# A two-batch product in the fill of a conditioned-residual kernel, with rank terms added in PSUM

## The chip, the cores and the metric

The kernel runs on one core of one Trainium2 chip. The metric is device time in microseconds (us) of one launch, as a median of runs. A profiled execution also has a span, from its first to its last instruction.

## What is computed

For each of 8 batches the reference builds a 512 x 512 matrix from a conditioning row and adds two residual layers to x (1024 x 512 per batch). Cut to what matters:

```python
h = gelu(layernorm(cond) @ w1 + b1)
x_a, x_b = split(h @ w2 + b2)                  # each (8, 512, RANK=8)
layer = base_layer + einsum('bdr,bkr->bdk', x_a, x_b)
x1 = x + (x + x @ layer)                       # first layer and its residual
ys = cond / sqrt(512)
d = rsqrt(ys**2 @ weight**2 + eps)
out = x1 + (x1 * ys) @ weight * d              # second layer and its residual
```

The kernel folds both layers into one matrix for each batch, P_b = (2I + base + A_b B_b) N_b with N_b = I + diag(ys_b) weight diag(d_b), and computes out_b = x_b P_b. Every product is done in fp32r with each factor as a rounded head and a remainder, so one product is three matmuls: head by head, head by remainder, remainder by head.

## The kernel before, in words

The work has two stages. In the **fill**, the P of the first batches is made while w2 (16 MB) streams in. In the **main** stage, 48 output tiles of batches 0 to 5 are made, twelve matmuls each, with other work hung on numbered tiles; batches 6 and 7 follow in a closing stage.

**The part of P without its rank term**, called q here, is (2I + base) N_b: 512 x 512 x 512, 48 matmuls of 128 x 512 for one batch. `Base` (lines 524-545) does it plainly: 16 units of three matmuls, and ScalarE copies each finished PSUM bank into `q[b]`. The class `Fill` (695-715) runs batches 1, 2 and 3 in this way (batch 0 was done ahead, `first_base`). `Pair` (547-643) makes q of two batches at once with seven products of half-size blocks in place of eight: 14 units of six matmuls for two batches. Its right operands are sums of blocks of N_b and N_b+1 (`sums`), rounded on ScalarE and completed on VectorE (`round`, `finish`); its left operands are sums of blocks of 2I + base^T, made by `left_sum` for products 5, 6, 3 and 7 (368-379). Before the change batches 4 and 5, and the parts for 6 and 7, use it from the main stage, and `left_sum` runs at the end of the fill (lines 800 to 804).

**What q still lacks.** Batch 0 was started before d was known, so `q[0]` holds only (2I + base) diag(ys) weight diag(d), and the identity's share of N_0 is missing: `twice_i_plus_base` and `add_base` (476-483) add 2I + base, from a copy of base (1 MB, `b_nat`), to `q[0]` on VectorE. Then the rank term: a matmul of two folded factors lands in a PSUM bank, and VectorE adds the bank to q: `rank_first` (497-501) for batch 0, `rank_term` (514-522) for the others, which first needs the folded factors loaded by eight small DMAs from POOL's queue (`load_rank`, 505-512). Then `split_p` (651-657) writes the head `ph` (ScalarE) and the remainder `pl` (VectorE) of P.

**x.** `load_x` brings half a batch (1 MB, SP's queue). `split_x` (667-674) cuts it in pieces of 256 columns: head on ScalarE, remainder on VectorE. Output tile t of the main stage uses piece t // 2, and its third matmul is the first to read the remainder (`main`, 811-821).

**What sets the order.** Matmuls keep their program order throughout (`mm`, line 44). In the fill, VectorE, ScalarE and SP keep theirs too (`InOrder`, 52-64), so the list in lines 717 to 805 is an order written by hand for each of these queues; after `InOrder.on = False` (805) their instructions are placed by the scheduler of the framework. POOL's DMAs are placed by it everywhere. In the main loop (1003-1014) `at(place, f)` hangs work behind tile number `place`. `rank_t` (435-470) is a generator: each `next(steps)` issues one step of the chain for the factor B. `w2_group` (389-403) loads 1 MB of w2 and issues eight matmuls of 32 columns with it.

**Buffers.** PSUM has four `acc` banks, two `misc` banks and two `px` banks in the fill; the last four become the `po` banks of the main stage when `setup` closes (807). Tiles of 1 MB share nine slots called `big`. Right operands share two slots each for heads (`nh`) and remainders (`nl`).

Of the kernel before, what the change touches and what calls it, by code (L numbers as in the profile page):

```python
# [30 lines left out]
def cond_resid_kernel(ctx: ExitStack, tc: tile.TileContext, small, cond, condrows, consts,  # L31
# [99 lines left out]

    def right_tiles(name):

        h = npool.tile([P, 2, D], F32R, tag="nh", name=f"nh_{name}")
        l = npool.tile([P, 2, D], F32R, tag="nl", name=f"nl_{name}")
        return h, l

    right0 = [right_tiles(f"0_{j}") for j in range(2)]
# [194 lines left out]
    def n_half(b, j):  # L333

        n = npool.tile([P, 2, D], F32, tag="n", name=f"n_{b}_{j}", bufs=4)
        for kk in range(2):
            k = 2 * j + kk
            ve.scalar_tensor_tensor(n[:, kk, :], w_sb[:, k, :], ysT[:, k, b:b + 1],
                                           d_all[b], ALU.mult, ALU.mult)
            blk = n[:, kk, k * P:(k + 1) * P]  # L340
            ve.tensor_add(blk, blk, ident)
        return n

    def round_right(n, name, wide=True):
# [20 lines left out]
    a11, a21 = b_raw[:, 0:2, 0:HD], b_raw[:, 0:2, HD:D]  # L365
    a12, a22 = b_raw[:, 2:4, 0:HD], b_raw[:, 2:4, HD:D]

    def left_sum(i):
        if i == 5:
            sraw["s"] = big_tile("sraw").rearrange("p k (u i) -> p k u i", u=2)  # L370
        s1, s2, s3, s4 = (sraw["s"][:, u] for u in range(4))
        s, x, y, op = {5: (s1, a21, a22, ve.tensor_add), 6: (s2, s1, a11, ve.tensor_sub),
                       3: (s4, a12, s2, ve.tensor_sub), 7: (s3, a11, a21, ve.tensor_sub)}[i]
        op(s, x, y)
        h = cp.tile([P, 2, HD], F32R, name=f"sh_{i}")
        l = cp.tile([P, 2, HD], F32R, name=f"sl_{i}")
        se.copy(h, s)
        ve.tensor_sub(l, s, h.bitcast(F32))
        left[i] = h, l

    b_nat = []


    px = [xps.tile([P, D], F32, name=f"px_{h}") for h in range(2)]
# [4 lines left out]
    def w2_group():  # L389
        h, r, k = todo.pop(0)  # L390
        t = big_tile(f"w2_{h}_{r}_{k}")
        sy.dma_start(t, w2[h, r, k])
        if len(todo) == 15:
            sy.dma_start(cst, consts)
        if len(todo) == 8:
            sy.dma_start(crow, condrows)
            sy.dma_start(b2r, b2rows)
        if len(todo) == 6:
            b_nat.append(big_tile("b_nat"))
            sy.dma_start(b_nat[0], base)  # L400
        for j in range(4):
            mm(px[h][32 * j:32 * j + 32, :], hT[:, k, r, :], t[:, j, :],
               start=(r == 0 and k == 0), stop=(r == 1 and k == KC - 1))
# [69 lines left out]

        ve.tensor_mul(q[b][:, c, :], q[b][:, c, :], d_all[b])

    def twice_i_plus_base():
        for c in range(KC):
            blk = b_nat[0][:, c, c * P:(c + 1) * P]
            ve.scalar_tensor_tensor(blk, ident, 2.0, blk, ALU.mult, ALU.add)

    def add_base(b):
        for c in range(KC):
            ve.tensor_add(q[b][:, c, :], q[b][:, c, :], b_nat[0][:, c, :])

    def round_w(k):
        se.copy(wh[:, k, :], w_sb[:, k, :])
# [7 lines left out]
        tm[0] = sp.tile([P, D], F32R, name="tm_0")  # L494
        ve.tensor_scalar_mul(tm[0], stt[0].bitcast(F32), mask[:, 0:1])

    def rank_first(c):

        ps = misc.tile([P, D], F32, tag="misc", name=f"pr_0_{c}")
        mm(ps, sa[0][:, c * P:(c + 1) * P], tm[0], start=True, stop=True)  # L500
        ve.tensor_add(q[0][:, c, :], ps, q[0][:, c, :])

    fold = {}

    def load_rank(b):

        for name in ("a", "t"):
            g, i = divmod(b, 4)
            fold[name, b] = npool.tile([P, D], F32R, tag=f"f{name}", name=f"f{name}_{b}", bufs=2)
            for c in range(KC):  # L510
                nc.gpsimd.dma_start(fold[name, b][32 * c:32 * c + 32, :],  # L511
                                    kept[name, g][32 * i:32 * i + 32, :])

    def rank_term(b):

        ps = [acc.tile([P, D], F32, tag="acc", name=f"pr_{b}_{c}") for c in range(KC)]
        for c in range(KC):
            at = slice(32 * c, 32 * c + 32)
            mm(ps[c], fold["a", b][at, c * P:(c + 1) * P], fold["t", b][at, :],
               start=True, stop=True)  # L520
        for c in range(KC):
            ve.tensor_add(q[b][:, c, :], ps[c], q[b][:, c, :])

    class Base:

# [21 lines left out]
    class Pair:  # L547
# [60 lines left out]
                    mm(bank, a[:, kk, at], m[:, kk, :], start=(first and kk == 0 and i == 0),  # L608
                       stop=(kk == 1 and i == 2), skip_group_check=not first)

        def unit(self):
            p, s = self.todo.pop(0)
            b, w, z = self.b, ("w", s), ("z", s)
            key = w if p in (1, 6, 7, 4) else z
            first = p in (1, 5, 2)
            if first:
                self.bank[key] = acc.tile([P, D], F32, tag="acc", name=f"pp_{b}_{p}_{s}")
            if (p, s) in ((1, 0), (6, 0)):
                i = b + (p == 6)
                q[i] = big_tile(f"q_{i}")  # L620
            bank = self.bank[key]
            self.product(p, s, bank, first)
            c11, c21 = q[b][:, s, :], q[b][:, 2 + s, :]
            c12, c22 = (q[b + 1][:, s, :], q[b + 1][:, 2 + s, :]) if b + 1 in q else (None, None)
            if p == 1:
                se.copy(c11, bank)
            elif p == 5:
                se.copy(c21, bank)
            elif p == 6:
                se.copy(c12, bank)  # L630
            elif p == 3:
                ve.tensor_add(c12, bank, c12)
            elif p == 7:
                se.copy(c22, bank)
                ve.tensor_add(c22, c22, c21)
            elif p == 2:
                ve.tensor_add(c11, bank, c11)
            else:
                se.copy(c21, bank)
# [27 lines left out]
    def split_x(b, j, part=None):  # L667
# [3 lines left out]
            xs[b, j] = big.tile([P, 2, KC, 2 * P], F32R, tag="big", name=f"xs_{b}_{j}")  # L671
            se.copy(xs[b, j][:, 0], t)
        if part != 0:
            ve.tensor_sub(xs[b, j][:, 1], t, xs[b, j][:, 0].bitcast(F32))


    stt, sa = [None, None], [None, None]
# [14 lines left out]
    bcast_d(0)  # L692
    first_base(3, (1, 2, 3))

    class Fill:


        def __init__(self):
            self.bases = [Base(b) for b in (1, 2, 3)]
            self.ns, self.rests = {}, {}  # L700

        def units(self, count):
            for _ in range(count):
                if self.bases[0].at == 4 * KC:
                    self.bases.pop(0)
                self.bases[0].units(1)

        def make_n(self, b, j):
            self.ns[b, j] = n_half(b, j)

        def round(self, b, j):
            self.rests[b, j] = round_right(self.ns[b, j], f"{b}_{j}", b == 3)

        def finish(self, b, j):
            next(f for f in self.bases if f.b == b).add(self.rests[b, j]())

    fill = Fill()
    fill.make_n(1, 0)
    fill.round(1, 0)
    fill.make_n(1, 1)  # L720
    keep_first((0, 1))
    fill.round(1, 1)
    keep_first((2, 3))
    fill.finish(1, 0)
    for c in range(2):
        times_d(0, c)
    fill.finish(1, 1)
    for c in range(2, KC):
        times_d(0, c)
    w2_group()  # L730
    w2_group()
    for k in range(2, KC):
        round_w(k)
    fill.units(4)
    for k in range(2, KC):
        rest_w(k)
    fill.make_n(2, 0)
    w2_group()
    w2_group()
    fill.units(4)  # L740
    fill.round(2, 0)
    fill.make_n(2, 1)
    fill.finish(2, 0)
    w2_group()
    w2_group()
    fill.units(6)
    w2_group()
    steps = rank_t()
    next(steps)
    w2_group()  # L750
    next(steps)
    fill.units(4)
    w2_group()
    next(steps)
    w2_group()
    fill.units(2)
    fill.round(2, 1)
    next(steps)
    fill.finish(2, 1)
    next(steps)  # L760
    fill.units(3)
    twice_i_plus_base()
    w2_group()
    next(steps)
    w2_group()
    next(steps)
    mask_t()
    add_base(0)
    fill.units(2)
    fill.make_n(3, 0)  # L770
    next(steps)
    w2_group()
    w2_group()
    next(steps)
    fill.units(2)
    w2_group()
    load_x(0, 0)
    xa = (split(with_bias(0)),)
    fill.round(3, 0)
    fill.units(4)  # L780
    done = stack(xa, neg_a, "a", 0)
    fill.finish(3, 0)
    sa[0] = done()
    fill.units(3)
    fill.make_n(3, 1)
    p_tiles(0)
    rank_first(0)
    rank_first(1)
    fill.round(3, 1)
    fill.units(2)  # L790
    split_p(0, 0, 0)
    rank_first(2)
    rank_first(3)
    split_p(0, 0, 1)
    fill.finish(3, 1)
    split_p(0, 1)
    split_x(0, 0)
    fill.units(4)
    sa[1] = stack(xa, neg_a, "a", 1)()
    left_sum(5)  # L800
    fill.units(8)
    split_x(0, 1)
    for p in (6, 3, 7):
        left_sum(p)
    InOrder.on = False

    setup.close()
    po = ctx.enter_context(tc.tile_pool(name="po", bufs=4, space=PSUM))
    pools = {"o": making.enter_context(tc.tile_pool(name="opool", bufs=4))}

    def main(b, t):
        s = xs[b, t // 2]
# [149 lines left out]

    pairs = {}
    place = lambda i: divmod(i, NTT)
    for b in range(1, 4):
        first = (b - 1) * NTT
        at(*place(max(0, 3 * b - 7)), load_rank, b)
        at(*place(3 * b - 1), rank_term, b)
        for j in range(2):
            at(*place(first + 3 + j), split_p, b, j)  # L970

    for b, spots in ((4, [11 + 3 * n // 4 for n in range(14)]), (6, [24 + 2 * n // 3 for n in range(14)])):
        first, end = spots[0], spots[-1] + 1
# [118 lines left out]
```

## Time and profile before

| | us |
|---|---|
| median of 3 runs (301.88 to 302.4) | 301.93 |
| the profiled execution | 302.08 |
| its span | 300.3 |
| matmuls of the fill's batches 1 to 3, first start | 26.68 |
| first matmul of the main stage | 80.35 |
| first matmul of the closing stage | 254.59 |

Matmul durations overlap in the profile: a matmul of 128 x 512 is listed with 0.39 to 0.40 us, and the next starts 0.23 us after it. Instructions of VectorE and ScalarE overlap by some 0.1 us in the same way, so queues are added up here by the distance of starts. "PE" is TensorE, "DVE" VectorE, "ACT" ScalarE.

### The profile page before, as it was taken

How to read it: one execution, taken by the hardware profiler on the slowest of the kernel's cores; microseconds unless marked ns; L12 is line 12 of the kernel's file. 1: busy time of each engine (PE TensorE's matmuls, PEld its weight loads, DVE VectorE, ACT ScalarE, POOL GpSimd, SP SyncE). 2: the span in 40 equal slices, each digit the busy share in tenths (PEclk: the TensorE clock that was granted, in tenths of full speed). 3: DMA queues.
4: the chain of work that ended last, by engine and by line, in shares of the span. 5: the costliest groups of instructions: out<-in, count | busy, mean ns of one | idle time of the engine just before them, and what ended most of it. 6: DMA issues, size and time to landing. Idle time of an engine off the chain costs nothing.

```text
span 300.3 us, 4005 instructions
## 1 busy us (share of the span) xinstructions
PE 293.4 (98%) x1501; PEld 227.1 (76%) x1501; DVE 211.0 (70%) x312; ACT 154.1 (51%) x226; POOL 34.8 (12%) x74
## 2 busy tenths in 40 slices
PE   7999999999999999999999999999999999999995
PEld 2655465466877778888887888888778888998995
DVE  4779840979569999935869994366562996479722
ACT  4757132256566673647634463656442663663630
POOL 0011000057004551000003600000000000000000
PEclk9999999999999999999999999999999999999999
DMA  7999999696619984605513841524516785131234
GB/s 210 410 428 419 405 424 419 219 326 183 197 70 305 306 288 126 239 35 210 204 43 97 230 164 46 201 55 192 210 70 210 244 267 227 38 140 49 93 140 142
DMA packets 19524, 62.14 MB, mean 207 GB/s; under 512 B 2720, under 2 KB 4000, under 8 KB 15152
## 3 DMA queue, kind: packets, MB, share of 16 engines
q1 hardware_dynamic: 6896, 39.57, 35.7%
q10 hardware_dynamic: 8832, 15.99, 14.2%
q0 software_dynamic: 3776, 6.31, 8.0%
q8 instruction: 12, 0.20, 0.3%
q14 instruction: 8, 0.07, 0.1%
HBM read 44.02 MB, written 17.84 MB: 206 GB/s over the span
## 4 chain that ended last, share of the span: by engine, by line
PE 84%; DVE 9%; ACT 3%; DMA 2%; issue 1%; SPq 0%; ACTq 0%
PE po L45 44%; PE pp L45 13%; PE pq L45 10%; PE sw L45 5%; PE px L45 4%; PE sz L45 2%; PE pg L45 2%; DVE n L62 2%; DMA b_raw<-in_baseT 2%; DVE sraw L62 1%; PE pr L45 1%; PE sv L45 1%; ACT o L62 1%; DVE sl L62 1%; ACT sh L62 1%
## 5 line engine op out<-in xcount | busy, mean ns | idle before, releaser
L45 PE MATMUL po<-ph,xs 128*128 128x512 f32 x384 | 123.8, 392 | 0.0
L45 PEld LDWEIGHTS po<-ph,xs 128*128 128x128 f32 x384 | 72.1, 188 | 16.8 <-issue 1.7
L45 PE MATMUL po<-pl,xs 128*128 128x512 f32 x192 | 74.8, 389 | 0.0
L62 ACT COPY o<-po 128x512 f32<-128x512 f32 x48 | 28.1, 586 | 52.8 <-PE po L45 52.8
L45 PEld LDWEIGHTS po<-pl,xs 128*128 128x128 f32 x192 | 36.1, 188 | 7.4
L62 DVE TENSOR_TENSOR xs<-x,xs 128x1024 fp32r<-128x1024 f32 x24 | 29.0, 1221 | 10.5 <-ACT xs L62 10.4
L62 ACT CAST xs<-x 128x1024 fp32r<-128x1024 f32 x24 | 24.9, 1052 | 3.7 <-DMA x<-in_x 1.9
L62 DVE TENSOR_TENSOR nl_p<-n,nh_p 128x1024 fp32r<-128x1024 f32 x14 | 17.1, 1222 | 12.3 <-ACT nh_p L62 12.2
L62 DVE TENSOR_TENSOR pl<-q,ph 128x1024 fp32r<-128x1024 f32 (+1 forms) x16 | 18.3, 1153 | 6.2 <-ACT ph L62 6.1
L62 DVE TENSOR_TENSOR q<-pr,q 128x512 f32<-128x512 f32 x32 | 20.1, 682 | 3.5 <-PE pr L45 3.5
L511 POOL DMA_DIRECT2D fa<-kept_a x28 | 13.7, 502 | 64.9 <-PE pr L45 64.8
L45 PE MATMUL pq<-nh,bh 128*128 128x512 f32 x48 | 19.8, 412 | 0.0
L45 PE MATMUL pq<-nl,bh 128*128 128x512 f32 x48 | 19.1, 398 | 0.1
L45 PE MATMUL pq<-nh,bl 128*128 128x512 f32 x48 | 19.0, 395 | 0.0
L62 DVE SCALAR_TENSOR_TENSOR n<-w_sb,ysT,d 128x512 f32<-128x512 f32 x24 | 17.7, 745 | 1.2 <-DMA d<-d_out 1.2
L62 ACT CAST nh_p<-n 128x1024 fp32r<-128x1024 f32 x14 | 14.8, 1054 | 6.3 <-PE pp L45 5.5
L62 ACT COPY o<-sw 128x512 f32<-128x512 f32 (+1 forms) x15 | 7.5, 500 | 19.2 <-PE sw L45 14.4
L62 ACT CAST ph<-q 128x1024 fp32r<-128x1024 f32 (+1 forms) x16 | 15.8, 1001 | 1.2 <-DVE q L62 0.8
L45 PE MATMUL px<-w,hT 128*32 128x512 f32 x128 | 16.0, 601 | 0.0
L62 ACT COPY q<-pp 128x512 f32<-128x512 f32 x20 | 11.7, 587 | 7.7 <-PE pp L45 7.7
L45 PEld LDWEIGHTS pq<-nh,bh 128*128 128x128 f32 x48 | 9.0, 188 | 8.4 <-issue 5.0
L511 POOL DMA_DIRECT2D ft<-kept_t x28 | 13.8, 509 | 5.2 <-DMA kept_t<-st_t 5.0
(185 smaller groups left out, 515.1 us busy)
## 6 DMA issues: line engine op xcount, KB each, us to landing
w<-in_w SPq DMA_DIRECT2D x16, 1024.0 KB, 10.5
x<-in_x SPq DMA_DIRECT2D x16, 1024.0 KB, 5.4
out<-o ACTq DMA_DIRECT2D x48, 256.0 KB, 3.2
out<-o ACTq DMA_DIRECT2D x6, 512.0 KB, 2.9
ft<-kept_t POOLq DMA_DIRECT2D x28, 64.0 KB, 3.4
fa<-kept_a POOLq DMA_DIRECT2D x28, 64.0 KB, 2.9
d<-d_out POOLq DMA_DIRECT2D x6, 256.0 KB, 5.2
w_sb<-in_weight SPq DMA_DIRECT2D x2, 512.0 KB, 5.3
```

The lines of the kernel that those rows point to most:

```text
L45: tc.keep_in_program_order(nc.tensor.matmul(*args, **kw))
L62: return lambda *a, **kw: pin(f(*a, **kw)) if InOrder.on else f(*a, **kw)
L511: nc.gpsimd.dma_start(fold[name, b][32 * c:32 * c + 32, :], kept[name, g][32 * i:32 * i + 32, :])
```

## The change

- **Batches 2 and 3** are made by `Pair(2)` in place of two `Base`. Twelve of its 14 units are in the fill, the last two (product 4) behind output tiles 1 and 2 of the main stage. All sums for the left operands are made in the middle of the fill (`left_raw`, `left_rest`). Two kinds of additions on VectorE can be put off with `unit(hold)`.
- **Right operands** have three slots in place of two.
- **Batch 0's base** is added by a DMA from POOL's queue that accumulates into `q[0]`; the copy `b_nat` and four additions on VectorE go.
- **Rank terms of batches 0, 1 and 2**: ScalarE copies q into the PSUM bank (`seed`), the matmul adds onto it, and `take` splits P straight out of the bank (head on ScalarE, remainder on VectorE). Addition into q and `split_p` go for these batches. Batch 3 keeps the old way. The rank terms of batches 1, 2 and 3 hang behind tiles 3, 9 and 6 (before: 2, 5 and 8), their loads behind 0, 4 and 1 (before: 0, 0 and 2). The folded factors get a pool of their own, opened when the fill ends.
- **Pieces 1 to 3 of batch 0's x**: the remainder is made by ScalarE writing minus the head, and an accumulating DMA from POOL's queue adding x from DRAM.
- `n_half` adds the identity to both of its blocks in one instruction.

The core of the diff:

```diff
-        h = npool.tile([P, 2, D], F32R, tag="nh", name=f"nh_{name}")
-        l = npool.tile([P, 2, D], F32R, tag="nl", name=f"nl_{name}")
+        h = npool.tile([P, 2, D], F32R, tag="nh", name=f"nh_{name}", bufs=3)
+        l = npool.tile([P, 2, D], F32R, tag="nl", name=f"nl_{name}", bufs=3)
...
-            blk = n[:, kk, k * P:(k + 1) * P]
-            ve.tensor_add(blk, blk, ident)
+        blk = n.rearrange("p k (c i) -> p (k c) i", i=P)[:, 2 * j:2 * j + 6:5, :]
+        ve.tensor_add(blk, blk, ident.unsqueeze(1).to_broadcast([P, 2, P]))
...
+    def add_base():
+
+        blk = q[0].rearrange("p k (c i) -> p (k c) i", i=P)[:, 0:16:5, :]
+        ve.scalar_tensor_tensor(blk, ident.unsqueeze(1).to_broadcast([P, KC, P]), 2.0, blk,
+                                ALU.mult, ALU.add)
+        nc.gpsimd.dma_start(q[0], base, accum_op=ALU.add)
...
+    def seed(b, c, ps):
+        se.copy(ps, q[b][:, c, :])
+    def take(b, c, ps):
+        se.copy(ph[b][:, c, :], ps)
+        ve.tensor_sub(pl[b][:, c, :], ps, ph[b][:, c, :].bitcast(F32))
+    def onto(ps, a, t):
+        mm(ps, a, t, start=False, stop=True, skip_group_check=True)
...
+            hi, lo = xs[b, j][:, 0], xs[b, j][:, 1]
+            if b == 0 and j:
+                se.mul(lo, hi.bitcast(F32), -1.0)
+                nc.gpsimd.dma_start(lo, x[b, j // 2][:, :, (j % 2) * 2 * P:(j % 2 + 1) * 2 * P],
+                                    accum_op=ALU.add)
...
+    two = Pair(2)
+    two.make_n(1)
     w2_group()
     w2_group()
-    fill.units(4)
+    base1.units(4)
+    two.round(1)
+    two.make_n(2)
+    two.round(2)
+    left_raw(5)
+    two.finish(1)
+    left_raw(6)
+    left_rest(5)
+    left_raw(7)
+    left_raw(3)
+    left_rest(6)
+    add_base()
...
+    bank = [px[1], misc.tile([P, D], F32, tag="misc", name="pr_0_1")]
+    p_tiles(0)
+    for c in range(2):
+        seed(0, c, bank[c])
+    two.unit()
+    two.finish(3)
     w2_group()
     load_x(0, 0)
     xa = (split(with_bias(0)),)
+    two.units(2)
     done = stack(xa, neg_a, "a", 0)
+    bank.append(px[0])
+    seed(0, 2, bank[2])
+    two.round(7)
     sa[0] = done()
+    bank.append(misc.tile([P, D], F32, tag="misc", name="pr_0_3"))
+    seed(0, 3, bank[3])
+    two.finish(7)
+    held = []
+    two.unit(held)
+    for c in range(KC):
+        rank_first(c, bank[c])
+        take(0, c, bank[c])
     split_x(0, 0)
+    two.unit(held)
+    two.unit(held)
+    two.unit(held)
     sa[1] = stack(xa, neg_a, "a", 1)()
+    two.round(4)
+    two.finish(4)
+    for f in held:
+        f()
     split_x(0, 1)
-    for p in (6, 3, 7):
-        left_sum(p)
     InOrder.on = False
...
+    at(*place(1), two.unit)
+    at(*place(2), two.unit)
+    for b, load, spot in ((1, 0, 3), (3, 1, 6), (2, 4, 9)):
+        at(*place(load), load_rank, b)
+        at(*place(spot), rank_term, b, b < 3)
+    for j in range(2):
+        at(*place(19 + j), split_p, 3, j)
```

More of the change, by code (lines that the diff above doesn't have):

```diff
@@ L366, in cond_resid_kernel, with left_raw @@
     a12, a22 = b_raw[:, 2:4, 0:HD], b_raw[:, 2:4, HD:D]
-    def left_sum(i):
+    def left_raw(i):
         if i == 5:
@@ L375, in left_sum, with left_rest @@
         h = cp.tile([P, 2, HD], F32R, name=f"sh_{i}")
+        se.copy(h, s)
+        sraw[i] = s, h
+    def left_rest(i):
+        s, h = sraw[i]
         l = cp.tile([P, 2, HD], F32R, name=f"sl_{i}")
-        se.copy(h, s)
         ve.tensor_sub(l, s, h.bitcast(F32))
         left[i] = h, l
-    b_nat = []
     px = [xps.tile([P, D], F32, name=f"px_{h}") for h in range(2)]
@@ L397, in w2_group @@
             sy.dma_start(b2r, b2rows)
-        if len(todo) == 6:
-            b_nat.append(big_tile("b_nat"))
-            sy.dma_start(b_nat[0], base)
         for j in range(4):
@@ L474, in times_d @@
         ve.tensor_mul(q[b][:, c, :], q[b][:, c, :], d_all[b])
[L476 to L483, printed above, removed]
+    def add_base():
[3 more added lines that the diff above has]
+        nc.gpsimd.dma_start(q[0], base, accum_op=ALU.add)
     def round_w(k):
@@ L495, in mask_t, with rank_first @@
         ve.tensor_scalar_mul(tm[0], stt[0].bitcast(F32), mask[:, 0:1])
[L497 to L503, printed above, removed]
+    def seed(b, c, ps):
[5 more added lines that the diff above has]
+        mm(ps, a, t, start=False, stop=True, skip_group_check=True)
+    def rank_first(c, ps):
+        onto(ps, sa[0][:, c * P:(c + 1) * P], tm[0])
+    fold, pools = {}, {}
     def load_rank(b):
@@ L508, in load_rank @@
             g, i = divmod(b, 4)
-            fold[name, b] = npool.tile([P, D], F32R, tag=f"f{name}", name=f"f{name}_{b}", bufs=2)
+            fold[name, b] = pools["fold"].tile([P, D], F32R, tag=f"f{name}", name=f"f{name}_{b}", bufs=2)
             for c in range(KC):
@@ L512, in load_rank, with rank_term @@
                                     kept[name, g][32 * i:32 * i + 32, :])
-    def rank_term(b):
+    def rank_term(b, take_p=False):
         ps = [acc.tile([P, D], F32, tag="acc", name=f"pr_{b}_{c}") for c in range(KC)]
+        if take_p:
+            for c in range(KC):
+                seed(b, c, ps[c])
         for c in range(KC):
             at = slice(32 * c, 32 * c + 32)
-            mm(ps[c], fold["a", b][at, c * P:(c + 1) * P], fold["t", b][at, :],
-               start=True, stop=True)
+            a, t = fold["a", b][at, c * P:(c + 1) * P], fold["t", b][at, :]
+            if take_p:
+                onto(ps[c], a, t)
+            else:
+                mm(ps[c], a, t, start=True, stop=True)
         for c in range(KC):
-            ve.tensor_add(q[b][:, c, :], ps[c], q[b][:, c, :])
+            if take_p:
+                take(b, c, ps[c])
+            else:
+                ve.tensor_add(q[b][:, c, :], ps[c], q[b][:, c, :])
     class Base:
@@ L609, in product, with unit @@
                        stop=(kk == 1 and i == 2), skip_group_check=not first)
-        def unit(self):
+        def unit(self, hold=None):
             p, s = self.todo.pop(0)
@@ L630, in unit @@
                 se.copy(c12, bank)
+            elif p == 3 and hold is not None:
+                hold.append(lambda: ve.tensor_add(c12, bank, c12))
             elif p == 3:
@@ L634, in unit @@
                 se.copy(c22, bank)
-                ve.tensor_add(c22, c22, c21)
+                if hold is not None:
+                    hold.append(lambda: ve.tensor_add(c22, c22, c21))
+                else:
+                    ve.tensor_add(c22, c22, c21)
             elif p == 2:
@@ L673, in split_x @@
         if part != 0:
-            ve.tensor_sub(xs[b, j][:, 1], t, xs[b, j][:, 0].bitcast(F32))
+            hi, lo = xs[b, j][:, 0], xs[b, j][:, 1]
[3 more added lines that the diff above has]
+                                    accum_op=ALU.add)
+            else:
+                ve.tensor_sub(lo, t, hi.bitcast(F32))
     stt, sa = [None, None], [None, None]
@@ L693, in cond_resid_kernel, with round1 @@
     first_base(3, (1, 2, 3))
[L695 to L720, printed above, removed]
+    base1, n1 = Base(1), {}
+    def round1(j):
+        n1[j] = round_right(n1[j], f"1_{j}", False)
+    n1[0] = n_half(1, 0)
+    round1(0)
+    n1[1] = n_half(1, 1)
     keep_first((0, 1))
-    fill.round(1, 1)
+    round1(1)
     keep_first((2, 3))
-    fill.finish(1, 0)
+    base1.add(n1[0]())
     for c in range(2):
         times_d(0, c)
-    fill.finish(1, 1)
+    base1.add(n1[1]())
     for c in range(2, KC):
@@ L733, in cond_resid_kernel @@
         round_w(k)
-    fill.units(4)
+    base1.units(4)
     for k in range(2, KC):
         rest_w(k)
-    fill.make_n(2, 0)
+    two = Pair(2)
+    two.make_n(1)
     w2_group()
     w2_group()
[L740 to L743, printed above, removed]
+    base1.units(4)
+    two.round(1)
[9 more added lines that the diff above has]
+    add_base()
     w2_group()
     w2_group()
-    fill.units(6)
+    base1.units(6)
     w2_group()
@@ L749, in cond_resid_kernel @@
     next(steps)
+    left_rest(7)
     w2_group()
     next(steps)
-    fill.units(4)
+    base1.units(2)
+    left_rest(3)
+    two.finish(2)
+    two.unit()
+    two.make_n(5)
     w2_group()
     next(steps)
+    two.round(5)
+    two.finish(5)
     w2_group()
-    fill.units(2)
-    fill.round(2, 1)
+    two.unit()
     next(steps)
-    fill.finish(2, 1)
     next(steps)
-    fill.units(3)
-    twice_i_plus_base()
+    two.unit()
+    two.make_n(6)
+    two.unit()
     w2_group()
     next(steps)
+    two.round(6)
     w2_group()
@@ L767, in cond_resid_kernel @@
     mask_t()
-    add_base(0)
-    fill.units(2)
-    fill.make_n(3, 0)
+    two.unit()
+    two.finish(6)
     next(steps)
@@ L773, in cond_resid_kernel @@
     w2_group()
+    two.round(3)
     next(steps)
-    fill.units(2)
+    bank = [px[1], misc.tile([P, D], F32, tag="misc", name="pr_0_1")]
+    p_tiles(0)
+    for c in range(2):
+        seed(0, c, bank[c])
+    two.unit()
+    two.finish(3)
     w2_group()
@@ L778, in cond_resid_kernel @@
     xa = (split(with_bias(0)),)
-    fill.round(3, 0)
-    fill.units(4)
+    two.units(2)
     done = stack(xa, neg_a, "a", 0)
-    fill.finish(3, 0)
+    bank.append(px[0])
+    seed(0, 2, bank[2])
+    two.round(7)
     sa[0] = done()
[L784 to L796, printed above, removed]
+    bank.append(misc.tile([P, D], F32, tag="misc", name="pr_0_3"))
[3 more added lines that the diff above has]
+    two.unit(held)
+    for c in range(KC):
+        rank_first(c, bank[c])
+        take(0, c, bank[c])
     split_x(0, 0)
-    fill.units(4)
+    two.unit(held)
+    two.unit(held)
+    two.unit(held)
     sa[1] = stack(xa, neg_a, "a", 1)()
-    left_sum(5)
-    fill.units(8)
+    two.round(4)
+    two.finish(4)
+    for f in held:
+        f()
     split_x(0, 1)
-    for p in (6, 3, 7):
-        left_sum(p)
     InOrder.on = False
@@ L808, in cond_resid_kernel @@
     po = ctx.enter_context(tc.tile_pool(name="po", bufs=4, space=PSUM))
-    pools = {"o": making.enter_context(tc.tile_pool(name="opool", bufs=4))}
+    pools["fold"] = making.enter_context(tc.tile_pool(name="folds", bufs=2))
+    pools["o"] = making.enter_context(tc.tile_pool(name="opool", bufs=4))
     def main(b, t):
@@ L964, in cond_resid_kernel @@
     place = lambda i: divmod(i, NTT)
[L965 to L970, printed above, removed]
+    at(*place(1), two.unit)
[5 more added lines that the diff above has]
+        at(*place(19 + j), split_p, 3, j)
     for b, spots in ((4, [11 + 3 * n // 4 for n in range(14)]), (6, [24 + 2 * n // 3 for n in range(14)])):
```

## The prediction, on record before the result was known

> **What bounds the kernel now.** I read the page's busy table first, then the windows by stage, the chain of waits, and the timeline around the end of the fill.
>
> ```profile
> span 300.3 us, 4005 instructions
> ...
> PE 293.4 (98%) x1501; PEld 227.1 (76%) x1501; DVE 211.0 (70%) x312; ACT 154.1 (51%) x226; POOL 34.8 (12%) x74
> ```
>
> The matmul engine is the bound. The windows (columns PE, PEld, DVE, ACT, POOL, each with its instruction count, then clock, DMA share and GB/s) say where room is left in the fill:
>
> ```profile
> 22.00:43.00 21.00, 20.79 (x118) 11.32 (x118) 16.25 (x30) 8.26 (x15) 1.13 (x2) 1.00 1.01 415
> 43.00:63.40 20.40, 20.40 (x116) 10.93 (x112) 11.71 (x22) 5.21 (x9) 0.74 (x2) 1.00 0.88 344
> 63.40:80.40 17.00, 16.78 (x74) 12.94 (x71) 14.31 (x19) 10.32 (x15) 10.44 (x21) 1.00 0.72 217
> ```
>
> PE hardly stops. Up to 63.4, when the last group of w2 is used, DVE has 41.4 - 16.25 - 11.71 = 13.4 us free; after that only 2.7. The chain of waits (start, us, what) prices matmuls in a stream:
>
> ```profile
> 71.84 2.78 PE pq L45 x12
> ...
> 80.52 8.19 PE po L45 x36
> ...
> 115.23 2.80 PE pp L45 x12
> ```
>
> Twelve matmuls take 2.78 us, so **0.232 us each**; an output tile takes 2.73, a pair's unit of six 1.39. The timeline at the fill's end shows a chain that is harmless now:
>
> ```profile
> 74.45 0.40 PE L45 MATMUL ps_a<-work,sel 128*128 128x512 f32 x1
> ...
> 74.94 0.59 ACT L62 CAST work<-ps_a 128x512 fp32r<-128x512 f32 x1 [0.33 <-PE ps_a L45]
> ...
> 77.03 0.74 DVE L62 SCALAR_TENSOR_TENSOR st_a<-work,cst,ps_a 128x512 fp32r<-128x512 f32 x1
> ...
> 81.03 1.05 ACT L62 CAST xs<-x 128x1024 fp32r<-128x1024 f32 x1
> ...
> 82.12 1.23 DVE L62 TENSOR_TENSOR xs<-x,xs 128x1024 fp32r<-128x1024 f32 x1 [2.37 <-ACT xs L62]
> ```
>
> The last two rows are x's piece 1, complete at 83.35. Output tile 2 reads its head at 80.35 + 2 x 2.73 = 85.8 and its remainder 0.46 later, at **86.3**: 2.9 us of slack. The DMA table (last column: us from issue to landing):
>
> ```profile
> x<-in_x SPq DMA_DIRECT2D x16, 1024.0 KB, 5.4
> ...
> fa<-kept_a POOLq DMA_DIRECT2D x28, 64.0 KB, 2.9
> d<-d_out POOLq DMA_DIRECT2D x6, 256.0 KB, 5.2
> ...
> kept_a<-st_a POOLq DMA_DIRECT2D x2, 256.0 KB, 3.1
> ```
>
> **What the Trainium skill says.** (1) "DMA: Bandwidth & Descriptors", "Anatomy of one DMA": a POOL-issued DMA takes 2.0 us and its bytes at 436 GB/s. For 64 KB that is 2.15; the trace has 2.0 at the least, 2.9 in the median, so it is a floor. For 512 KB it gives an estimate of 3.2. (2) "Collectives: The Full Stack", "The bandwidth ceiling": an add in the DMA path needs two source reads and runs at about half the rate of a copy. No accumulating DMA is in this trace. (3) "PSUM — Partial Sum Buffer", "The four PSUM rules": a matmul without the start flag adds onto what ScalarE wrote where an earlier matmul set the bit. So a seed costs a ScalarE copy and no extra matmul; unseen here. (4) "TensorE: Matmul & The Clock Gate", "Back-to-back issue gap": 131 or 216 ns for 512 columns; the trace has 232 for this type, and that decides.
>
> **The change part by part.** *Matmuls.* Two plain batches are 2 x 48 = 96 matmuls; the pair is 14 x 6 = 84. Twelve fewer: 12 x 0.232 = **-2.78**. In the fill it is 24 fewer (-5.56), since two units (+2.78) move behind tiles 1 and 2.
>
> *DVE and ACT up to 63.4.* DVE gains, by distance of starts (0.60 for 128x512, 1.14 for 128x1024): left sums 8 x 0.60 = 4.8; wide remainders of five right operands in place of four narrow ones, 5.7 - 2.4 = 3.3; two right-hand sums 2.3; two adds from PSUM 1.3; a fourth half of N, 1.9; it loses 4 x 0.2 + 4 x 0.6 for base and gets one instruction of 0.65. Net +11.0 against 13.4 free. I walked through the queues in order: DVE reaches the sum of w2's first half at 43.2 (42.3 now), the last half at 64.3 (63.5), and PE, which has units queued at each point, ends the last w2 group at 63.2 (63.4). Cost **0**; were the cover gone, up to 1. Merging identity blocks gains 0.1 a half, on no path. The third slot for right operands makes each rounding find a free slot: from the walk, product 3's is free from 54.3, wanted at 62; 0. Slots of 1 MB: `b_nat` leaves, the left sums come earlier, `b_raw` is free by 42 instead of 90, so w2 comes no later.
>
> *Base by DMA.* 1 MB as before, on POOL's queue instead of SP's, issued near 43.3; first needed by a seed at 63. POOL has nothing between 28 and 57. Twenty us hide it; **0**.
>
> *The end of the fill.* After 63.2 PE needs products 6, 3, 7 (6 x 1.39 = 8.3), four rank matmuls and two stacks (1.4): 72.9. ACT now has seeds (4 x 0.55) and takes in its queue, so three waits come: the factor A for the rank matmul (split, stack, ACT, DVE) at 68.3 when PE is there at 67.9; the fourth seed behind product 7's rounding, 69.7 against 69.0; 0.3 at the stack itself. PE's second stack then runs near 74.2 and the main stage may start at **74.4** instead of 80.35: -5.9 (-5.56 of matmuls, -0.3 of PE waits on misc banks in the old rank terms and the like).
>
> *What is late next.* x's piece 1 stands last in the list, behind product 4's operand. From the stack at 74.2: ACT's two copies to 75.5; DVE's st_a1 to 76.3; the sum for product 4 to 77.4; ACT's rounding to 78.5; the cast of piece 1 to 79.45; its negation (unseen; the same size of cast is 1.05, a scaled ACT write of 128x512 is 0.71 against 0.62, so 1.0 to 1.2) to 80.55. Only then does POOL issue the accumulating DMA, 512 KB in rows of 1 KB. PE, started at 74.4, does two tiles and one unit and wants this remainder at 74.4 + 5.46 + 1.39 + 0.46 = **81.7**. Queued behind that matmul is everything on PE. Let L be issue to landing. The wait is 80.55 + L - 81.7. Product 4's operand itself is ready at 79.7, wanted at 79.9: 0. Should the `po` bank that still holds the second stack delay the start to 76.3, the wait shrinks by as much: the sum stays.
>
> *L.* Below: 2.0, the shortest POOL landing in the trace; it can't be less than a smaller plain one. Above: 7.5, from x's 5.4 for 1 MB (an add reads twice) and 2 for DRAM rows of 1 KB and other traffic. I take 5.0, between the skill's plain 3.2 and twice the bytes with contention; 256 KB of d takes 5.2.
>
> *Later rank terms.* Batches 1 and 2: four seeds and eight takes on ACT, DVE about 2.4 less each; hung where banks are free and five to seven tiles (14 us) before use. ACT is at 51%: 0; at worst a set of seeds late, 2.2. Pieces 2 and 3 are wanted 13 us and more after the fill: 0.
>
> *Sum.* Against now, the remainder of tile 2 arrives at 80.55 + L instead of 86.3, and one more unit follows: change = 80.55 + L - 86.3 + 1.39 = **L - 4.36**. At L = 5.0: +0.64. Profiled time 302.08 + 0.64 = 302.72; the median stands 0.15 lower: **302.6**.
>
> **The rivals.** *The accumulate is quick* (faster). For it: POOL's 64 KB land in 2.0 to 2.9, and DRAM and queues are quiet there. Against it: eight times the bytes, read twice. At L = 2.9, -1.46: **300.5**; with no wait at all 301.93 - 5.9 + 2.78 = 298.8. It decides from L = 4.36 down, or if the fill's end comes earlier by as much. *POOL's queue is the bound* (slower): `load_rank(1)` issues eight DMAs there (the eight at 71.27 took 3.96), free to go from the fill's end; ahead of the accumulate they add up to 4: about **305**. Against: the accumulate is earlier in the program. *DVE is late in the fill*: 11.0 of 13.4 us of room is used; blocked by ACT waits two or three more times at 0.7 it delays the fill and the tail by 1.5: **304.1**. That batch 0's additions go from DVE is sure; that the time is less, isn't.
>
> **How the numbers follow.** Forecast (a stall that gives the gain back): 0.47; its own range, L 3.8 to 6.5, is 301.4 to 304.1. Quick accumulate: 0.33. POOL's queue: 0.11. Late DVE: 0.09. Range: from 298.8 by 0.2 (a little of the quick case is left out) to 305.0, the top of the others: 299.0 to 305.0. About 0.2%, 0.6 us, can be told from no change. Faster: 0.31 of the quick case and 0.01 of the forecast, 0.32. Same: L 3.8 to 5.0, 0.20. Slower: 0.48.
>
> **What would show it.** Twelve fewer matmuls of 128x512; the main stage starting near 74.4 (to 76.3); DVE over 80% busy from 30 to 64; the accumulating DMA for piece 1 issued near 80.6, PE idle on it in tile 2 for some 4 us, and no other wait of PE over 1 us. A first tile after 76.5, a landing under 4 us, or a PE wait on seeds or banks would each prove a step wrong.

## The result, and the profile after

The changed kernel takes **321.17 us** in the median (318.96 to 321.78, 6 runs), the kernel before 302.08 beside it (301.82 to 302.56, 6 runs): ratio **1.0612, interval 1.0573 to 1.0650**, slower. 302.6 was forecast, within 299.0 to 305.0. The profiled spans are 320.0 and 300.3, so 19.7 us are to be found. The page's head, PE's busy line and the clock row:

```profile
span 320.0 us, 3998 instructions
...
PE 296.1 (93%) x1489; PEld 227.1 (71%) x1489; DVE 208.0 (65%) x293; ACT 166.2 (52%) x250; POOL 39.6 (12%) x78
...
PEclk9999998699996999999999999999999999999999
```

The twelve matmuls are gone, yet PE's busy time rose by 2.7 us: the 6s in the clock row (slices of 8 us) say that some products ran slowly. PE's share fell from 98 to 93%: it waits. The same windows as before (columns as there):

```profile
22.00:43.00 21.00, 19.72 (x109) 11.05 (x109) 20.02 (x34) 10.91 (x19) 1.57 (x3) 1.00 0.91 322
43.00:63.40 20.40, 13.34 (x59) 7.74 (x60) 8.59 (x12) 4.07 (x7) 0.46 (x1) 0.83 1.00 349
```

In the second, PE is busy 13.3 of 20.4 us where it was busy throughout, and DVE has 11.8 us free: the engine that the prediction had watched most is not short of time. The DMA engines are fully busy there. PE's waits from 20 us on name the releasers:

```profile
PE px L45 <- DMA w<-in_w: 8.0, 3, 5.1
PE po L45 <- DMA xs<-in_x: 7.8, 2, 6.3
PE po L45 <- DVE st_a L62: 1.7, 1, 1.7
```

Before, the largest entry of this list from 20 us on was (0.6 us at a time):

```profile
PE sw L45 <- ACT o L62: 1.1, 3, 0.6
```

**Where 19.7 us went** (distances between the starts of PE's products beyond their price, by the timeline; so counted, a wait is up to 0.2 us longer than in the list):

| stretch | us |
|---|---|
| fill: 24 matmuls fewer | -5.6 |
| fill: three waits for w2 (1.36, 1.80, 5.20) | +8.4 |
| fill: products at half speed behind the longest | +2.4 |
| fill: wait for the bank of the second stack | +1.9 |
| fill: waits for `st_a` and a seed 0.9, less the 1.4 of the old order's waits that are gone, rest 0.3 | -0.2 |
| main stage begins at 87.22, was 80.35 | **+6.9** |
| two units behind tiles 1 and 2 | +2.8 |
| tile 2: wait for x's piece 1 | +6.4 |
| tile 2: products at half speed behind it | +2.0 |
| tile 6: wait for piece 3 | +1.7 |
| from the main stage's start to the end | **+12.8** |

A *stack* (`stack`) is a product that lays one factor of the rank terms out for four batches. It ends in a `misc` bank, which stays taken until VectorE has written the remainder (`st_a`, `st_t`). The second stack of A is the last of the fill, and its bank is one of those that the main stage waits for.

### The profile page after: what moved, and what is told of

It reads as the page before. It is cut to its first block, busy times and chain, and to the rows that moved or that the text cites. A ratio compares the mean times of both kernels' runs of the same rounds, so it can differ in the third digit from the quotient of the medians.

```text
span 320.0 us, 3998 instructions
## 1 busy us (share of the span) xinstructions
PE 296.1 (93%) x1489; PEld 227.1 (71%) x1489; DVE 208.0 (65%) x293; ACT 166.2 (52%) x250; POOL 39.6 (12%) x78
## 3 DMA queue, kind: packets, MB, share of 16 engines
q0 software_dynamic: 5504, 8.93, 12.2%
## 4 chain that ended last, share of the span: by engine, by line
PE 74%; DMA 13%; DVE 5%; ACT 4%; issue 2%; POOL 0%; ACTq 0%; SPq 0%; POOLq 0%
PE po L45 38%; PE pp L45 17%; PE sw L45 6%; DMA w<-in_w 4%; DMA xs<-in_x 3%; PE sz L45 3%; PE px L45 2%; DMA fa<-kept_a 2%; PE warm L45 2%; DMA d<-d_out 2%; DMA d_out<-scr 2%; PE pg L45 2%; PE sv L45 1%; DVE n L62 1%; DVE sraw L62 1%
## 5 line engine op out<-in xcount | busy, mean ns | idle before, releaser
L62 DVE TENSOR_TENSOR nl_p<-n,nh_p 128x1024 fp32r<-128x1024 f32 x21 | 25.7, 1224 | 17.6 <-ACT nh_p L62 17.5
L62 ACT CAST nh_p<-n 128x1024 fp32r<-128x1024 f32 x21 | 22.1, 1053 | 13.2 <-DVE n L62 11.6
L62 ACT COPY q<-pp 128x512 f32<-128x512 f32 x30 | 17.6, 587 | 21.6 <-PE pp L45 21.6
L45 PE MATMUL pp<-nh_p,sh 128*128 128x512 f32 x48 | 19.1, 397 | 0.0
L45 PE MATMUL pp<-nl_p,sh 128*128 128x512 f32 x48 | 18.7, 390 | 0.0
L45 PE MATMUL pp<-nh_p,sl 128*128 128x512 f32 x48 | 18.7, 390 | 0.0
L62 DVE TENSOR_TENSOR q<-pr,q 128x512 f32<-128x512 f32 x20 | 12.5, 684 | 8.4 <-PE pr L45 8.4
L62 DVE TENSOR_TENSOR pl<-q,ph 128x1024 fp32r<-128x1024 f32 (+1 forms) x10 | 11.1, 1116 | 6.4 <-ACT ph L62 6.4
L45 PE MATMUL pp<-nh_p,bh 128*128 128x512 f32 x36 | 14.9, 414 | 0.0
L62 DVE TENSOR_TENSOR n<-n,n 128x1024 f32<-128x1024 f32 x12 | 14.7, 1224 | 0.1
```

The lines of the kernel that those rows point to most:

```text
L45: tc.keep_in_program_order(nc.tensor.matmul(*args, **kw))
L62: return lambda *a, **kw: pin(f(*a, **kw)) if InOrder.on else f(*a, **kw)
```

## The experiments

Two theories stood for the fill. *Slots*: the 1 MB slot that w1 frees at 16.05 went to a w2 load before and goes to `sraw` now, so loads 6 to 10 come late. *DMA*: the base's addition, in flight from 42.6 to 56.7, slows the w2 loads beside it. SP's waits (10 to 60 us) show the first, on `b_raw`'s slot (freed by DVE's `sraw` rows):

```profile
SPq L62 <- DVE sraw L62: 8.2, 1, 8.2
...
SPq L62 <- DVE sl L62: 3.2, 1, 3.2
```

Load 6 is issued at 20.93 (before: 16.05), load 10 at 41.12 (32.03). SP's timeline, before and after (three loads are merged in each line, which starts with load 6):

```profile
16.05 11.09 SPq L62 DMA_DIRECT2D w<-in_w  x3
...
20.93 10.42 SPq L62 DMA_DIRECT2D w<-in_w  x3
```

The windows of 5 us show the second; 45 to 55 us of the kernel before, then of the changed one to 60:

```profile
45.00:50.00 5.00, 5.00 (x31) 2.46 (x30) 0.14 (x1) 1.91 (x4) 0.00 (x0) 1.00 1.01 418
50.00:55.00 5.00, 5.00 (x27) 3.21 (x25) 2.85 (x5) 0.62 (x1) 0.00 (x0) 1.00 0.99 411
```

```profile
45.00:50.00 5.00, 3.37 (x20) 1.74 (x18) 4.74 (x7) 1.17 (x2) 0.00 (x0) 1.00 0.97 285
50.00:55.00 5.00, 0.63 (x8) 0.39 (x4) 1.23 (x1) 1.53 (x2) 0.00 (x0) 0.91 1.02 283
55.00:60.00 5.00, 4.22 (x14) 2.08 (x15) 0.00 (x0) 0.00 (x0) 0.00 (x0) 0.50 1.01 421
```

The DMA share (second to last) is the same, the bytes are a third fewer while the addition runs. Four kernels, beside 302.52 for the kernel before, told these apart.

**1. Left sums in place of their blocks** (no `sraw` slot; two of the sums change places in the order):

```diff
-        s, x, y, op = {5: (s1, a21, a22, ve.tensor_add), 6: (s2, s1, a11, ve.tensor_sub),
-                       3: (s4, a12, s2, ve.tensor_sub), 7: (s3, a11, a21, ve.tensor_sub)}[i]
+        s, x, y, op = {5: (a22, a21, a22, ve.tensor_add), 7: (a21, a11, a21, ve.tensor_sub),
+                       6: (a11, a22, a11, ve.tensor_sub), 3: (a12, a12, a11, ve.tensor_sub)}[i]
```

> The sums for the left operands are written over the blocks of b_raw, so they take no 1 MB slot. Slot theory (the sums took the slot that the sixth load of w2 had, and w2 comes late from there on): loads 6 and 10 of w2 are issued near 16 and 32 us instead of 20.9 and 41.1, the three waits of PE for w2 (8.0 us) shrink to under 2, and the time falls from 321 to about 311 to 313. DMA theory (the accumulating load of base slows the w2 stream that it runs beside): the waits stay within 2 us of 8.0 and the time stays above 318.

313.07 us, ratio 1.0357 (1.0328 to 1.0385): 8 us less than the changed kernel. Load 6 is issued at 16.31, load 10 at 35.84, the main stage starts at 78.95. PE's waits:

```profile
PE po L45 <- DMA xs<-in_x: 7.9, 2, 6.4
PE po L45 <- DVE st_a L62: 1.7, 1, 1.7
PE px L45 <- DMA w<-in_w: 1.5, 2, 0.8
```

w2's 8.0 fell to 1.5, x's stayed. Load 10 came later than the expected 32; the waits for w2 are under 2 all the same.

**2. Without the base's addition** (the base of batch 0 is left out of its q):

```diff
-        nc.gpsimd.dma_start(q[0], base, accum_op=ALU.add)
```

> Leaves out the accumulating DMA of base into batch 0 (so batch 0 lacks base), nothing else. DMA theory: w2's loads 11 to 13 land some 5 us sooner, the waits of PE for w2 fall from 8.0 to under 3, time 311 to 315. Slot theory: load 10 is still issued at 41 us, so the first two waits (2.9 us) and most of the third stay; time 317 to 321.

313.13 us, 1.0355 (1.0337 to 1.0373), though load 10 is still issued at 40.42; the DMA engines move 405 to 428 GB/s between 45 and 60 us, and the w2 waits are 2.8 us. So each theory is half of it: **either cause alone is mostly covered, both together make the 5.1 us wait**. The late slots use up the lead of the stream, and the addition then slows what is left of it. The time and the waits that each theory gave for its own kernel came true (313.07 at the very edge of 311 to 313), and each number that needed the other theory to be wrong failed.

**3. x's remainders on VectorE** (batch 0, as before):

```diff
-            if b == 0 and j:
-                se.mul(lo, hi.bitcast(F32), -1.0)
-                nc.gpsimd.dma_start(lo, x[b, j // 2][:, :, (j % 2) * 2 * P:(j % 2 + 1) * 2 * P],
-                                    accum_op=ALU.add)
-            else:
-                ve.tensor_sub(lo, t, hi.bitcast(F32))
+            ve.tensor_sub(lo, t, hi.bitcast(F32))
```

> Remainders of x's pieces 1 to 3 of batch 0 on VectorE again, no accumulating DMA for them. If these DMAs are what output tiles 2 and 6 wait for, the 7.8 us of waits go but for 1 to 2 us (VectorE does piece 1 after the held additions), and with them the slower clock after the long wait (tile 2's rest took 1.8 us longer): 321 to about 312. Rival, VectorE is the next limit there: a wait of 4 us or more of PE on VectorE's remainder in tile 2, time above 315. The w2 waits stay at about 8.

309.87 us, 1.0256 (1.0219 to 1.0293): 11.3 us less. No product waits for x; from the main stage's start to the end it takes 222.4 us, not 232.8. VectorE is in nobody's way: after the 1.7 us for the bank at the main stage's start, as in the changed kernel, PE waits for it nowhere. The w2 waits are 6.4 us, where about 8 were expected:

```profile
PE px L45 <- DMA w<-in_w: 6.4, 2, 5.8
```

**4. All three**, the base loaded on SP's queue and added by four VectorE instructions, as before the change but behind right operand 5:

```diff
-        nc.gpsimd.dma_start(q[0], base, accum_op=ALU.add)
+        for c in range(KC):
+            ve.tensor_add(q[0][:, c, :], q[0][:, c, :], b_nat[0][:, c, :])
```

> All three causes away: left sums over b_raw, base by a plain load and four additions on VectorE, x's remainders on VectorE. If the three causes add up, 321 - 10 (w2 waits and the clock after them) - 9 (x waits and the clock after them) = about 302; if the fill then ends near 76 as its matmul count allows, 299 to 301. If VectorE becomes the bound of the fill once it has all this work, the main stage starts after 80 and the time is 304 or more.

304.18 us (303.39 to 305.54), 1.0063 (1.0038 to 1.0087), the main stage from 79.18. 17 of the 19 us are back. What is still late is order in the fill: 1.7 for the second stack's bank, 1.6 for a w2 load, 1.1 ahead of T's stack.

**5. Copies in place of additions** (302.43 for the kernel before, here and in 6 to 8):

```diff
-        nc.gpsimd.dma_start(q[0], base, accum_op=ALU.add)
+        nc.gpsimd.dma_start(q[0], base)
...
-                nc.gpsimd.dma_start(lo, x[b, j // 2][:, :, (j % 2) * 2 * P:(j % 2 + 1) * 2 * P],
-                                    accum_op=ALU.add)
+                nc.gpsimd.dma_start(lo, x[b, j // 2][:, :, (j % 2) * 2 * P:(j % 2 + 1) * 2 * P])
```

> The four DMAs that add (the base of batch 0, three x remainders) are plain copies of the same sizes from the same places, on the same queue and behind the same waits; the addition is left out, so q of batch 0 and three remainders hold wrong values. If the adding itself is dear (each 512 KB addition takes 8.8 us, and the 1 MB one holds the w2 stream at some 284 GB/s), the copies land in under 6 us and some 10 us, the wait of tile 2 for xs falls from 6.3 to below 4 and the time to 313 to 317. If the route is dear (GpSimd's queue, the strided source, other loads at the same time), the landings stay within 1 us of 8.8 and 14.1 and the time stays at 320 to 322.

314.62 us (1.0401, 1.0369 to 1.0433). Landings (last column) of the changed kernel, then of this one:

```profile
w<-in_w SPq DMA_DIRECT2D x16, 1024.0 KB, 13.7
xs<-in_x POOLq DMA_DIRECT2D x3, 512.0 KB, 8.8
q<-in_base POOLq DMA_DIRECT2D x1, 1024.0 KB, 14.1
```

```profile
w<-in_w SPq DMA_DIRECT2D x16, 1024.0 KB, 11.2
xs<-in_x POOLq DMA_DIRECT2D x3, 512.0 KB, 4.7
q<-in_base POOLq DMA_DIRECT2D x1, 1024.0 KB, 10.0
```

The base takes 4.1 us less as a copy, and beside it, from 45 to 55 us, the engines move 421 and 423 GB/s where they moved 285 and 283 beside the addition. PE's w2 waits fall from 8.0 to 5.2, and were 2.8 with no transfer of base at all (experiment 2): the adding and the megabyte itself cost the w2 stream about the same. x's pieces 1, 2 and 3 land in 7.4, 4.7 and 3.8 us as copies, in 8.8, 7.3 and 10.3 with the addition, in different traffic; the medians alone hide that piece 1 gains only 1.4. PE still waits 4.8 for it: "below 4" failed. This piece shares the engines with a 1 MB load of x, issued 1.9 us ahead of it, and with stores and `fa` loads. That this traffic is the larger part of its 8.8 us is likely, as the other two copies land sooner, but not shown: no run took it away.

**6. The fourth kernel, three places of the fill moved.** The second stack of A goes two units earlier; the other two moves change places of one unit and one stack:

```diff
+    sa[1] = stack(xa, neg_a, "a", 1)()
     two.unit(held)
     two.unit(held)
-    sa[1] = stack(xa, neg_a, "a", 1)()
```

> The kernel of the fourth experiment (left sums in place, remainders of x and the base on VectorE), with three places of the fill moved: the second stack of A one unit behind the first rank terms rather than three, one unit of the pair ahead of the w2 group that waited 1.6 us, and the first stack of T one w2 group later. If the waits that were left there (1.9 for a bank, 1.7 for w2, 1.3 for the stack's operands) are stalls of order alone, some 4 us go: 299.5 to 301, below the kernel before (302.5). If they only hide a later limit (DVE, or the w2 stream), the time stays at 303 to 304.

302.85 us, 1.0013 (1.0006 to 1.0020): between the two expectations. The bank's and w2's waits are gone, but PE now waits 1.6 + 0.2 us ahead of T's stack and 1.5 ahead of A's:

```profile
PE ps_t L45 <- issue: 1.6, 1, 1.6
PE ps_a L45 <- DVE work L62: 1.5, 1, 1.5
```

"issue" names no engine, but the stack starts 0.1 us behind a cast on ScalarE, and that cast had waited for VectorE, which was at the four additions of the base (2.4 us) first.

**7. The same with the rank terms of batches 1 and 2 as before:**

```diff
-        at(*place(spot), rank_term, b, b < 3)
+        at(*place(spot), rank_term, b)
...
+        at(*place(4 + j), split_p, 1, j)
+        at(*place(11 + j), split_p, 2, j)
```

> As e6_best, but the rank terms of batches 1 and 2 are done as in the kernel before: product into an empty bank, VectorE adds it onto q, and ScalarE and VectorE split P out of q later. If seeds and takes lie beside TensorE's work, as predicted (0), the ratio to e6_best is within 0.2%; if they hold banks or ScalarE at tiles 3 and 9, e7_oldrank is faster by over 0.5 us.

302.86 us against 302.85: seeds and takes of these batches cost and bring **nothing** that can be told. Those of batch 0, in the fill, were undone in no run.

**8. The changed kernel with TensorE kept busy in tile 2:**

```diff
+        if (b, t) == (0, 2):
+            for n in range(26):
+                mm(ps, xs[0, 0][:, 0, 0, 0:P], ph[0][:, 0, :], start=True, stop=True)
```

> The changed kernel with 26 extra products of 512 columns (6.0 us at 0.232) into the bank of tile 2 of batch 0, ahead of its own, which then begin it anew: TensorE works through the 6.3 us in which it waited for xs. If the granted clock falls because TensorE idled, it stays above 0.95 in the 5 us behind that place, and the 2 us that those products lost come back: 1.5 to 2.5 us less than the changed kernel in the span from the main stage's start. If the clock falls for another reason, it falls there too (0.75 or so), and the time stays or grows by some tenths.

318.58 us (1.0529, 1.0482 to 1.0575). The window 100 to 105 us of the changed kernel, then of this one; the clock is the third figure from the end:

```profile
100.00:105.00 5.00, 3.92 (x9) 3.15 (x10) 0.00 (x0) 0.00 (x0) 2.93 (x6) 0.50 1.22 238
```

```profile
100.00:105.00 5.00, 4.24 (x19) 3.45 (x19) 0.50 (x1) 1.56 (x3) 3.24 (x7) 1.00 1.18 231
```

0.50 becomes 1.00: **the fall of the clock comes from the idle time**. From the main stage's start to the end of tile 2 it takes 16.67 us, not 18.18, so 1.5 come back; 0.8 of it goes again at tile 6, whose wait grows to 2.3. The span from the main stage's start shrinks by 0.75 only, less than I expected.

**9. The sixth kernel, VectorE's order in the fill changed** (302.36 before):

```diff
     two.round(6)
+    base_rows((0, 1))
...
-    two.finish(3)
     w2_group()
     load_x(0, 0)
     xa = (split(with_bias(0)),)
+    two.finish(3)
+    base_rows((2, 3))
```

> As e6_best, with three pieces of work of VectorE moved off the path of the rank chain: the four additions of the base in two pairs (behind the rounding of right operand 6 and behind the split of A, not ahead of T), and the split of A ahead of the remainder of right operand 3. If the order on VectorE is all that is left in the fill (1.6 + 0.2 us ahead of the stack of T, 1.5 ahead of the stack of A), the main stage starts at 76 and the time is 299.5 to 301. If VectorE is simply full there, the waits come back elsewhere and the time stays at 302.4 to 303.2.

301.67 us (300.56 to 303.01, 22 runs), **ratio 0.9978, interval 0.9968 to 0.9988**: faster than the kernel before by 0.2%, short of the 299.5 to 301 expected. The main stage starts at 77.83; the two longest waits left in the second half of the fill are:

```profile
PE px L45 <- DVE st_a L62: 1.6, 1, 1.6
...
PE px L45 <- DMA w<-in_w: 0.6, 1, 0.6
```

The waits ahead of T's and A's stacks are gone. Behind the first of these two, some seven products are 0.43 us apart.

**10. The ninth, `st_a` ahead of right operand 7** (302.41 before):

```diff
-    two.round(7)
     sa[0] = done()
...
+    two.round(7)
     two.finish(7)
```

> As e9_best2, with one pair of lines exchanged: the remainder st_a of the first stack of A goes ahead of right operand 7 on VectorE and ScalarE, so that it comes at 69.1 and not at 70.2. If the 1.6 us that TensorE waits for it, and the ten slow products behind that wait (0.43 us apart and not 0.23, some 2 us), are what still keeps the fill long, the main stage starts at 75 to 76 (77.8 in e9_best2) and the time is 299.0 to 300.5. If the wait passes on to right operand 7 (nl_p late by 1 us), it is 301 to 302.

303.19 us (301.4 to 304.88), 1.0017 (0.9998 to 1.0036). The 1.6 us wait fell to 0.4, and one of 2.1 us came up at the second stack, whose bank is free only when VectorE has taken batch 0's P out of it:

```profile
PE ps_a L45 <- DVE pl L62: 2.1, 1, 2.1
```

Neither expectation was right: the wait moved, to a bank. Part of the time is the clock: in nine of the 14 executions the mean granted clock was 0.992 to 0.994 and the median 303.22, in the other five 0.999 or more and 301.67.

## Why the prediction was wrong, step by step

- **Matmuls**, -2.78 over the run: right (1489 for 1501), and the moved units cost their 2.78 behind tiles 1 and 2.
- **DVE and ACT up to 63.4, 0**: right as to the engines. DVE was over 80% busy to 50 us and PE lost nothing to it. DVE's own fall to near none from 51 to 60 is the stall, not its cause.
- **"`b_raw` is free by 42 instead of 90, so w2 comes no later": failed.** I counted slots and not the order in which they are claimed. `sraw` takes the slot of 16.05 in its turn, SP's queue then stands 8.2 us at `b_raw`'s, and what is queued behind it is the rest of w2. "Free by 42" was right (41); load 10 had gone out at 32.
- **"Twenty us hide it; 0" for the base: failed.** The seed that reads it never waited. I priced the transfer by its reader and not by what it runs beside: the w2 stream, whose engines the kernel before already filled at 0.99 to 1.01. The note drawn on for the accumulate's bound (the Trainium skill, "Collectives: The Full Stack", "The bandwidth ceiling": about half the rate, of the add step of a collective) belonged in this step too; here the total fell from about 415 to 284 GB/s beside the addition.
- **End of fill, main stage from 74.4 to 76.3**: failed by 11 to 13 us, of which w2 with the slow products behind it is 10.8. The small waits foreseen there came (0.5 for the factor A, 0.4 for the fourth seed), and the po bank did delay the start, by 1.9, the case named.
- **The chain to piece 1: right as a mechanism.** The timeline after:

```profile
85.11 0.40 PE L45 MATMUL ps_a<-work,sel 128*128 128x512 f32 x1
...
90.87 1.07 ACT L62 ACTIVATE xs<-xs 128x1024 fp32r<-128x1024 f32 x1
...
92.24 1.28 POOL L701 DMA_DIRECT2D xs<-in_x  x1 [0.23 <-issue]
...
101.08 1.22 PE L45 MATMUL po<-ph,xs 128*128 128x512 f32 x2 [6.27 <-DMA xs<-in_x]
```

From the stack to the issue it took 7.1 us, 6.35 were predicted; the negation 1.07 (1.0 to 1.2). **L was mis-sized**: 8.8, above the upper bound of 7.5, for 5.0. The bound had 2 us for rows and other traffic and did not count the 1 MB load of x beside it; even the copy took 7.4.
- **The sum had no term for the clock.** The Trainium skill ("TensorE: Matmul & The Clock Gate", "HAM oscillation — how this bites in real kernels") warns of idle gaps over some 3.4 us, after which TensorE restarts at half its clock. The trace agrees at both long waits: granted 0.50, products 0.43 us apart for 0.23, worth 2.4 and 2.0 us. A forecast wait of 4 us should have carried that. The page's figure is no limit here, though: waits of 1.6 to 2.1 us had slow products behind them in three profiles (last section).
- **Later rank terms, 0**: right (experiment 7). **Pieces 2 and 3, 0**: failed, 1.7 us in tile 6: piece 3 took 10.3 us to land.
- **Rivals.** POOL's queue: three of the eight `fa` loads did go ahead (1.5 us), but the issue followed 0.3 us behind the negation, so its place in the queue decided nothing. Late DVE: refuted. The quick accumulate: refuted.
- **The prediction's own sum closes with these terms:** 0.6 forecast, 10.9 for the second stack (85.1 for 74.2), 0.8 for the chain, 3.8 for L, 2.0 for the clock in tile 2 and 1.7 for tile 6 make 19.8, where 19.7 was measured. The path was right; the two zeros for the w2 stream were the dear error.

## What to carry to other kernels

A transfer off the path has a price of its own: what else its engines would have moved in that time; look at the DMA share of its window before writing 0, and at GB/s after it: a full share moved a third fewer bytes here. When buffers rotate, walk the claims in program order to the next load in the queue: one early claim ahead of a stream holds all that stands behind it. Moving additions from a VectorE with room to a full DMA path gained nothing here: undone, with the pair kept and the fill put in order, the saved matmuls were worth 0.2%.

## What the runs showed of the hardware

- An addition by DMA landed later than the copy of the same bytes: 14.1 us against 10.0 for 1 MB (12.2 and 13.0 in experiments 1 and 3), 7.3 to 10.3 against 3.8 to 7.4 for 512 KB, each in its own traffic. With the DMA share at 0.97 to 1.02, the engines moved 283 to 285 GB/s beside the 1 MB addition and 421 to 423 beside the copy. POOL's issue of the 512 KB addition is longer too: 1.28 us for 0.80.
- A wait of 5 to 6 us halved the clock (0.50) for the next 4 to 5 us. Shorter waits did so in some profiles (1.6, 2.1 and 1.8 us in experiments 9, 10 and 7: products 0.43 us apart) and not in others (1.7 us in the changed kernel and the fourth, 1.6 in the sixth). It isn't the kernel alone that decides: of 22 executions of the ninth, eight had a mean clock of 0.993 to 0.994 (median 302.04) and 14 one of 0.998 or more (301.35). What does decide at that length stays open.
- A product into a bank that ScalarE has seeded adds onto the seed, at a seed of 0.60 us per 128x512.
